# Products between an attention's steps: column pieces of the attention's own shape, or whole 128-column matmuls

## The chip, the cores and the metric

The kernel runs on one core of a Trainium2 chip. A core has TensorE (matrix products, results in PSUM), VectorE, ScalarE, GpSimd and DMA queues, each with its own stream of instructions; semaphores order them. The metric is the device time of one execution in microseconds (us), median of several runs. TensorE's array has 128 rows (the contracted dimension, "active rows") and 128 columns (the outputs, "active columns"). A matmul that needs fewer rows or columns uses a part of the array, and several such matmuls on different parts can run side by side. In this document a *shape* such as 128\*32 is rows\*columns of one matmul, as the profile prints it.

## The reference, cut to what matters

The input is 16 images of 256 channels and 32 x 32 = 1024 positions, all in float32. Each image goes through two layers:

```python
# layer 0: attention with 4 heads of 64
xs = x.reshape(B, C, S).transpose(0, 2, 1)
qkv = (xs @ w_proj + b_proj).reshape(B, S, 4, 192)
q, k, v = jnp.split(qkv, 3, axis=-1)
attn = softmax(einsum('bihd,bjhd->bijh', q, k) * 64 ** -0.5, axis=2)
x = einsum('bijh,bjhd->bihd', attn, v).reshape(B, S, 256) @ w_out + b_out + xs
# layer 1: group norm, attention with 8 heads of 32, group norm, MLP 256 -> 1024 -> 256
x = x + attention(group_norm(x, gn1_w, gn1_b), qkv_w, proj_w, proj_b, phys_bias)
h = group_norm(x, gn2_w, gn2_b)
h = gelu(mlp_w1 @ h + mlp_b1)
x = x + (mlp_w2 @ h + mlp_b2)
```

## The kernel before: the parts that matter

The program runs image after image. An attention is a generator: each step emits the scores of some units (`s`), then weighs the values of the step before (`acc`), and yields; between two steps the caller runs deferred work (`later.tick()`) and, in the second attention, one piece of a list `fill`. D is 64 in the first attention and 32 in the second, and G = 128 / D heads share a tile. Scores contract over D rows, so their shape is 64\*128 or 32\*128 and G of them lie side by side in the array's rows. Weighing contracts over 128 positions and gives D columns, so its shape is 128\*64 or 128\*32, and G of them lie side by side in the columns.

```python
    cols = [P]                                   # P = 128

    def product(o, w, r, **flags):
        for c0 in range(0, P, cols[0]):
            sl = slice(c0, c0 + cols[0])
            nc.tensor.matmul(o[sl], w[:, sl], r, **flags)

    def attention(layer, b, D, qT, kT, v_of, ones_of, scale, project):
        # ... cut: items, units; a step is 6 // G units: 3 in the first attention, 1 in the second
        def scores(i, kb):
            # ... cut: PSUM tiles
            for g in range(G):
                nc.tensor.matmul(
                    tiles[g // 2][:, g % 2, :],
                    kT[g * D : (g + 1) * D, c, kb * P : (kb + 1) * P],
                    qT[g * D : (g + 1) * D, c, t * TB : (t + 1) * TB],
                    start=True,
                    stop=True,
                )
            # ... cut: ScalarE takes the exponentials e of each tile, 128 x 1024

        def weigh(i, kb, es):
            # ... cut
            for g in range(G):
                nc.tensor.matmul(
                    accs[i][g * D : (g + 1) * D, :],
                    v_of(c * G + g, kb),
                    es[g // 2][:, g % 2, :],
                    start=(kb == 0),
                    stop=(kb == SB - 1),
                )
            # ... cut: VectorE sums the exponentials; after the last kb: copy, later.after(2, normalise)

        # ... cut: normalise (matmuls den, shape as acc; then later.after(3, project))
        cols[0] = D
        pending = []
        for step in steps:
            now = [scores(*u) for u in step]
            for p in pending:
                weigh(*p)
            pending = now
            yield
        for p in pending:
            weigh(*p)
        yield
        cols[0] = P
```

So `product` gives one matmul over all 128 columns outside an attention, and 128 / D pieces over D columns inside one. These helpers use it: `out_proj` (profile names `o`, first attention, and `j`, second attention; each has 4 products of 512 moving columns), `group_norm` (`gm`, `gv`, two moving columns), `qkv` (`qk_a`, `v_a` for the first attention, `qk_b`, `v_b` for the second; 4 products of 512 or 8 of 256) and `reduce`, the MLP's second product (`m<-g`, 8 products of 256):

```python
        def reduce(t, co, half):
            n = TB // 2
            ps = wide(f"m2_{b}_{t}_{co}_{half}")[:, 0, :n]
            for hc in range(HC):
                product(
                    ps,
                    k["w2"][:, hc, co * P : (co + 1) * P],
                    gs[t, hc][:, half * n : (half + 1) * n],
                    start=(hc == 0),
                    stop=(hc == HC - 1),
                )
            # ... cut: VectorE adds bias and residual, DMA out
```

The MLP's first product (`m<-hn`) and `qk_b`, `v_b` run outside the attentions, whole. The order of the parts:

```python
    for b in range(B):
        # ... cut: load of the next image
        run(attention_0(b, tiles0, xs[b], ...))
        first_qkv = []
        if b + 1 < B:
            tiles0, first_qkv = qkv_0(b + 1, xs[b + 1])
        run_pieces(first_qkv if b == 0 else hidden)
        later.flush()
        fill = outputs + (first_qkv if b > 0 else [])
        last = NT * CC * SB - 1
        tiles1, second_qkv = qkv_1(b, xn)
        run_pieces(second_qkv)
        # ... cut
        run(
            attention_1(b, tiles1, xs[b], ...),
            {n * last // max(len(fill) - 1, 1): piece for n, piece in enumerate(fill)},
        )
        hidden, outputs = mlp(b, xs[b], hn)
    later.flush()
    run_pieces(hidden + outputs)
```

The second attention has 32 steps (`last` is 31). In it run, for images 1 to 14, the eight `reduce` pieces of the image before and the six pieces of q, k, v of the next image, at steps 0, 2, 4, 7, 9, 11, 14, 16, 19, 21, 23, 26, 28 and 31; image 15 has the eight alone, image 0 none.

Of the kernel before, what the change touches and what calls it, by code (L numbers as in the profile page):

```python
# [14 lines left out]
P = 128  # L15
# [175 lines left out]
def first_pass(ctx, tc, x, out, k):  # L191
    nc = tc.nc
    B, C, S = x.shape
    CC, SB, NT = C // P, S // P, S // TB
# [33 lines left out]

    cols = [P]

    def product(o, w, r, **flags):
        for c0 in range(0, P, cols[0]):
            sl = slice(c0, c0 + cols[0])
            nc.tensor.matmul(o[sl], w[:, sl], r, **flags)  # L236

# [4 lines left out]
    def attention(layer, b, D, qT, kT, v_of, ones_of, scale, project):  # L248
        key = f"{layer}_{b}"
        G = P // D  # L250
        items = [(t, c) for t in range(NT) for c in range(CC)]
        units = [(i, kb) for i in range(len(items)) for kb in range(SB)]
        per = 6 // G
        steps = [units[n : n + per] for n in range(0, len(units), per)]
        res = act.tile([P, CC, S], F32, tag="res", name=f"res_{key}")
        accs, held, sums = {}, {}, {}

        def scores(i, kb):
            t, c = items[i]
            tiles = [wide(f"s_{key}_{i}_{kb}_{n}") for n in range(G // 2)]  # L260
# [8 lines that stand above are left out]
            es = []  # L269
            for n, s in enumerate(tiles):  # L270
                e = work.tile(
                    [P, 2, TB], F32, tag="e", name=f"e_{key}_{i}_{kb}_{n}", bufs=8
                )
                nc.scalar.activation(e, s, AF.Exp, scale=scale)  # L274
                es.append(e)
            return i, kb, es

        def weigh(i, kb, es):
            t, c = items[i]
            if kb == 0:  # L280
                accs[i] = bank(f"acc_{key}_{i}")
# [8 lines that stand above are left out]
            if kb == 0:  # L290
                held[i] = es
                return
            if kb == 1:
                sums[i] = [
                    work.tile([P, 2, TB], F32, tag="es", name=f"es_{key}_{i}_{n}", bufs=4)
                    for n in range(G // 2)
                ]
            for n, e in enumerate(es):
                d = sums[i][n]
                nc.vector.tensor_add(d, held[i][n] if kb == 1 else d, e)  # L300
            if kb == SB - 1:
                r = res[:, c, t * TB : (t + 1) * TB]
                nc.scalar.copy(r, accs.pop(i))
                later.after(2, lambda: normalise(i, r))

        def normalise(i, r):
            t, c = items[i]
            den = bank(f"den_{key}_{i}")
            for g in range(G):
                nc.tensor.matmul(  # L310
                    den[g * D : (g + 1) * D, :],
                    ones_of(c * G + g),
                    sums[i][g // 2][:, g % 2, :],
                    start=True,
                    stop=True,
                )
            at = next(block)
            d = work.tile([P, TB], F32, tag="d", name=f"d_{key}_{i}", bufs=1)
            nc.scalar.activation(  # L319
                d, den, AF.Identity, accum_out=dsum[:, at : at + 1]  # L320
            )
            nc.scalar.activation(
                den, den, AF.Exp, scale=-1.0 / DEN_MIN, accum_out=lsum[:, at : at + 1]
            )
            nc.vector.reciprocal(d, d)  # L325
            nc.vector.tensor_mul(r, r, d)
            if c == CC - 1:
                later.after(3, lambda: project(t, res))

        cols[0] = D  # L330
        pending = []
        for step in steps:
            now = [scores(*u) for u in step]
# [4 lines that stand above are left out]
        for p in pending:  # L338
            weigh(*p)
        yield  # L340
        cols[0] = P


    def out_proj(key, w, nk, src, bias, xs, t, stats):
        ps = wide(f"{key}_{t}")
        for co in range(CC):
            for kc in range(nk):
                product(
                    ps[:, co, :],
                    w[:, kc, co * P : (co + 1) * P],  # L350
                    src(kc),
                    start=(kc == 0),
                    stop=(kc == nk - 1),
                )
        for co in range(CC):
            y = xs[:, co, t * TB : (t + 1) * TB]
            nc.vector.scalar_tensor_tensor(
                y, ps[:, co, :], bias[:, co : co + 1], y, ALU.add, ALU.add
            )
            if stats is not None:  # L360
                nc.vector.bn_stats(stats[:, co, t, :], y)


    def group_norm(key, src, stats, gw, gb, y):
        st = {}

        def means():
            mv = small.tile([P, CC, 2], F32, tag="mv", name=f"mv_{key}")
            for cc in range(CC):
                nc.vector.bn_aggr(mv[:, cc, :], stats[:, cc].rearrange("p t k -> p (t k)"))  # L370
            mean_c = small.tile([P, CC], F32, tag="mean_c", name=f"mean_c_{key}")
            nc.vector.tensor_copy(mean_c, mv[:, :, 0])
            st.update(mv=mv, mean_c=mean_c)
            later.after(1, variances)

        def variances():
            ps = bank(f"gm_{key}")
            product(ps[:, :CC], k["gavg"], st["mean_c"], start=True, stop=True)
            mean = small.tile([P, CC], F32, tag="mean", name=f"mean_{key}")
            nc.vector.tensor_copy(mean, ps[:, :CC])  # L380

            dv = small.tile([P, CC], F32, tag="dv", name=f"dv_{key}")
            nc.vector.tensor_sub(dv, st["mean_c"], mean)
            nc.vector.tensor_mul(dv, dv, dv)
            tv = small.tile([P, CC], F32, tag="tv", name=f"tv_{key}")
            nc.vector.tensor_add(tv, dv, st["mv"][:, :, 1])
            st.update(mean=mean, tv=tv)
            later.after(1, apply)

        def apply():  # L390
            ps = bank(f"gv_{key}")
            product(ps[:, :CC], k["gavg"], st["tv"], start=True, stop=True)
            rstd = small.tile([P, CC], F32, tag="rstd", name=f"rstd_{key}")
            nc.vector.tensor_scalar(rstd, ps[:, :CC], EPS, None, ALU.add)
            nc.gpsimd.tensor_tensor(rstd, rstd, k["mhalf"], ALU.pow)
            a = small.tile([P, CC], F32, tag="ga", name=f"ga_{key}")
            nc.vector.tensor_mul(a, rstd, gw)
            ma = small.tile([P, CC], F32, tag="gma", name=f"gma_{key}")
            nc.vector.tensor_mul(ma, st["mean"], a)
            c = small.tile([P, CC], F32, tag="gc", name=f"gc_{key}")  # L400
            nc.vector.tensor_sub(c, gb, ma)
            for t in range(NT):
                sl = slice(t * TB, (t + 1) * TB)
                for cc in range(CC):
                    nc.vector.tensor_scalar(  # L405
                        y[:, cc, sl], src[:, cc, sl],
                        a[:, cc : cc + 1], c[:, cc : cc + 1], ALU.mult, ALU.add,
                    )

        means()  # L410


    def qkv(key, D, src, weights, b_qk, b_v, v_op, qT, kT, v_dst):
        def qk(ch, which, dst):
            ps = wide(f"qk_{key}_{ch}_{which}")
            for t in range(NT):
                for cc in range(CC):
                    product(
                        ps[:, t, :],
                        weights(cc, which)[:, ch * P : (ch + 1) * P],  # L420
                        src[:, cc, t * TB : (t + 1) * TB],
                        start=(cc == 0),
# [10 lines left out]
        def v(half):  # L433
            ps = wide(f"v_{key}_{half}")
            n = SB // 2
            for i in range(n):
                sb = half * n + i
                o = ps[:, i // 2, (i % 2) * C : (i % 2 + 1) * C]
                for cc in range(CC):
                    product(  # L440
                        o,
                        src[:, cc, sb * P : (sb + 1) * P],
                        weights(cc, 2),
# [75 lines left out]
    def mlp(b, xb, hn):  # L519
# [20 lines left out]
        def reduce(t, co, half):  # L540
            n = TB // 2
            ps = wide(f"m2_{b}_{t}_{co}_{half}")[:, 0, :n]
            for hc in range(HC):
                product(
                    ps,
                    k["w2"][:, hc, co * P : (co + 1) * P],
                    gs[t, hc][:, half * n : (half + 1) * n],
# [371 lines left out]
```

## Time and profile before

| what | value |
|---|---|
| time, median of 3 runs | 4013.07 us (4011.88 to 4015.5) |
| span of the profiled execution | 4013.6 us |
| TensorE busy | 3971.1 us, 99% |
| TensorE records of matmuls | 27957 |
| VectorE, ScalarE busy | 2481.6 us (62%), 2078.1 us (52%) |
| scores of the second attention `s_b`, 4096 records | 624.3 us |
| weighing of the second attention `acc_b`, 4096 records | 546.1 us |
| `s_a`, `acc_a`, 2048 records each | 490.9 us, 477.5 us |

How to read it: a float32 matmul leaves two records. Busy time of a group counts time in which several of its records overlap once, so groups of small shapes have a mean duration well over busy time / count. A row of a timeline merges records of one kind that follow each other: start, time to the end of the last one, engine, line, operation, output<-inputs, shape, size of the moving operand, count. The end of a matmul record is modelled, and the next kind may start before it; the difference of two starts is what an operation holds TensorE for.

### The profile page before, as it was taken

Reading aid. Unit: us, or ns where it says so; the run is one execution under the profiler, and the core shown is the slowest. Engines: PE = TensorE matmul, PEld = TensorE weight load, DVE = VectorE, ACT = ScalarE, POOL = GpSimd, SP = SyncE. Lnnn points to the kernel's source line nnn. Section 1 sums busy time; section 2 is a strip of 40 time slices with the busy share of each in tenths; the row PEclk is TensorE's granted clock in tenths of the full one; section 3 lists DMA queues with packets and bytes.
Section 4 is the critical chain, followed back from the end, with each engine's and each line's share of the span. In section 5 each row is a group of like instructions: output and inputs, shape, how many; then the busy total and the mean of one; then the engine's idle time right before and its main releaser. Section 6 shows DMA issues by size and latency. Waiting matters only on the chain.

```text
span 4013.6 us, 64073 instructions
## 1 busy us (share of the span) xinstructions
PE 3971.1 (99%) x27957; PEld 1518.4 (38%) x27957; DVE 2481.6 (62%) x2538; ACT 2078.1 (52%) x2623; POOL 32.7 (1%) x54
## 2 busy tenths in 40 slices
PE   9999999999999999999999999999999999999998
PEld 3334343343433434334343343433434334343334
DVE  5684756847467474774747747476574765747563
ACT  4564545545455464554545545465454545646462
POOL 1000000000000000000000000000000000000000
PEclk9999999999999999999999999999999999999999
DMA  2000000000000000000000000000000000000000
GB/s 75 1 1 6 17 1 22 1 9 14 1 22 1 9 14 1 22 1 9 14 3 20 1 14 9 3 20 1 22 1 3 20 1 22 1 6 7 1 9 14
DMA packets 19872, 42.07 MB, mean 10 GB/s; under 512 B 5216, under 2 KB 6752, under 8 KB 19584
## 3 DMA queue, kind: packets, MB, share of 16 engines
q1 hardware_dynamic: 13824, 33.56, 2.3%
q8 instruction: 221, 3.62, 0.4%
q10 hardware_dynamic: 5296, 4.20, 0.4%
q14 instruction: 67, 0.55, 0.0%
q0 software_dynamic: 464, 0.15, 0.0%
HBM read 21.12 MB, written 16.78 MB: 9 GB/s over the span
## 4 chain that ended last, share of the span: by engine, by line
PE 94%; DVE 4%; issue 1%; ACT 0%; DMA 0%; POOL 0%; ACTq 0%; POOLq 0%; DVEq 0%
PE s_b L262 14%; PE acc_b L283 12%; PE m L527 11%; PE m L236 11%; PE s_a L262 11%; PE acc_a L283 11%; PE qk_a L236 6%; PE qk_b L236 6%; PE o L236 3%; PE v_b L236 3%; PE v_a L236 3%; PE j L236 3%; PE den_a L310 1%; PE den_b L310 1%; DVE d_a L325 1%
## 5 line engine op out<-in xcount | busy, mean ns | idle before, releaser
L274 ACT ACTIVATE e_b<-s_b 128x1024 f32<-128x1024 f32 x1024 | 994.0, 1025 | 660.6 <-PE s_b L262 648.1
L300 DVE TENSOR_TENSOR es_b<-es_b,e_b 128x1024 f32<-128x1024 f32 x768 | 888.7, 1216 | 147.8 <-ACT e_b L274 146.2
L262 PE MATMUL s_b<-q,k 32*128 32x512 f32 x4096 | 624.3, 640 | 2.8 <-DVE x L552 1.3
L274 ACT ACTIVATE e_a<-s_a 128x1024 f32<-128x1024 f32 x512 | 488.7, 1024 | 205.3 <-PE s_a L262 174.9
L283 PE MATMUL acc_b<-e_b,v 128*32 128x512 f32 x4096 | 546.1, 604 | 0.0
L262 PE MATMUL s_a<-q,k 64*128 64x512 f32 x2048 | 490.9, 608 | 0.0
L300 DVE TENSOR_TENSOR es_a<-es_a,e_a 128x1024 f32<-128x1024 f32 x384 | 467.2, 1217 | 36.0 <-ACT e_a L274 10.2
L527 PE MATMUL m<-hn,w 128*128 128x512 f32 x1024 | 476.1, 606 | 2.0 <-DVE hn L405 2.0
L283 PE MATMUL acc_a<-e_a,v 128*64 128x512 f32 x2048 | 477.5, 600 | 0.0
L236 PE MATMUL m<-g,w 128*32 128x256 f32 (+1 forms) x7808 | 464.9, 379 | 3.7 <-DVE v L448 3.7
L236 PEld LDWEIGHTS m<-g,w 128*32 128x32 f32 (+1 forms) x7808 | 272.6, 111 | 227.7 <-issue 59.3
L262 PEld LDWEIGHTS s_b<-q,k 32*128 32x128 f32 x4096 | 199.3, 183 | 368.4 <-issue 279.2
L535 ACT ACTIVATE g<-m,m1b 128x512 f32<-128x512 f32 x256 | 170.2, 685 | 315.7 <-PE m L527 315.2
L262 PEld LDWEIGHTS s_a<-q,k 64*128 64x128 f32 x2048 | 181.8, 186 | 282.4 <-issue 241.8
L527 PEld LDWEIGHTS m<-hn,w 128*128 128x128 f32 x1024 | 186.6, 191 | 257.1 <-issue 191.5
L448 DVE TENSOR_TENSOR v<-v_b,eones 128x1024 f32<-128x1024 f32 x32 | 39.2, 1224 | 394.4 <-PE v_b L236 394.4
L300 DVE TENSOR_TENSOR es_b<-e_b,e_b 128x1024 f32<-128x1024 f32 x128 | 151.1, 1222 | 188.6 <-ACT e_b L274 188.6
L325 DVE RECIPROCAL d_a<-d_a 128x512 f32<-128x512 f32 x64 | 214.6, 3353 | 83.1 <-ACT d_a L319 83.1
L283 PEld LDWEIGHTS acc_a<-e_a,v 128*64 128x64 f32 x2048 | 132.8, 136 | 322.2 <-issue 317.6
L236 PE MATMUL qk_a<-x,wp 128*32 128x512 f32 (+1 forms) x1856 | 234.3, 594 | 9.1 <-DMA wp<-in_L_conv_w_proj_dram 9.1
L236 PE MATMUL qk_b<-xn,wq 128*128 128x512 f32 x512 | 226.6, 596 | 3.3 <-DVE xn L405 3.3
L283 PEld LDWEIGHTS acc_b<-e_b,v 128*32 128x32 f32 x4096 | 82.5, 108 | 380.2 <-issue 376.0
(104 smaller groups left out, 2389.5 us busy)
## 6 DMA issues: line engine op xcount, KB each, us to landing
x<-in_x_dram SPq DMA_DIRECT2D x32, 512.0 KB, 4.5
out_dram<-x SPq DMA_DIRECT2D x64, 256.0 KB, 2.0
w<-in_L_conv_mlp_w_dram ACTq DMA_DIRECT2D x2, 1024.0 KB, 11.4
wp<-in_L_conv_w_proj_dram ACTq DMA_DIRECT2D x6, 128.0 KB, 8.5
wq<-in_L_conv_qkv_w_dram ACTq DMA_DIRECT2D x1, 768.0 KB, 8.9
wo<-in_L_conv_w_out_dram ACTq DMA_DIRECT2D x1, 256.0 KB, 5.2
wpj<-in_L_conv_proj_w_dram ACTq DMA_DIRECT2D x1, 256.0 KB, 10.6
bv<-in_L_conv_b_proj_dram POOLq DMA_DIRECT2D x1, 128.0 KB, 7.4
```

Of the source, the lines that this page charges most:

```text
L236: nc.tensor.matmul(o[sl], w[:, sl], r, **flags)
L262: nc.tensor.matmul(tiles[g // 2][:, g % 2, :], kT[g * D : (g + 1) * D, c, kb * P : (kb + 1) * P], qT[g * D : (g + 1) * D, c, t * TB : (t + ...
L274: nc.scalar.activation(e, s, AF.Exp, scale=scale)
L283: nc.tensor.matmul(accs[i][g * D : (g + 1) * D, :], v_of(c * G + g, kb), es[g // 2][:, g % 2, :], start=(kb == 0), stop=(kb == SB - 1),)
L300: nc.vector.tensor_add(d, held[i][n] if kb == 1 else d, e)
L310: nc.tensor.matmul(den[g * D : (g + 1) * D, :], ones_of(c * G + g), sums[i][g // 2][:, g % 2, :], start=True, stop=True,)
L325: nc.vector.reciprocal(d, d)
L448: nc.vector.tensor_tensor(v_dst[:, half * n : (half + 1) * n], ps.rearrange("p a (b h d) -> p (a b) h d", b=2, d=D), b_v.unsqueeze(1).to_b ...
L527: nc.tensor.matmul(ps[:, n, :], k["w1"][:, cc, hc * P : (hc + 1) * P], hn[:, cc, t * TB : (t + 1) * TB], start=(cc == 0), stop=(cc == CC - 1),
L535: nc.scalar.activation(g, ps[:, n, :], AF.Gelu, bias=k["m1b"][:, hc : hc + 1])
```

## The change

The helper `product` and its variable `cols` go away, and every product is one matmul over 128 columns, wherever it is emitted. Inside an attention this replaces four matmuls of 32 columns, or two of 64, with one of 128; the pieces, their places between the steps and everything on the other engines stay. It makes the kernel simpler and takes away instructions; in return these products no longer have the shape of the weighing that runs just ahead of them.

```diff
--- before.py
+++ after.py
@@ in first_pass @@
-    cols = [P]
-
-    def product(o, w, r, **flags):
-        for c0 in range(0, P, cols[0]):
-            sl = slice(c0, c0 + cols[0])
-            nc.tensor.matmul(o[sl], w[:, sl], r, **flags)
@@ in attention @@
-        cols[0] = D
         pending = []
         for step in steps:
 ... cut
         yield
-        cols[0] = P
@@ in out_proj @@
             for kc in range(nk):
-                product(
+                nc.tensor.matmul(
                     ps[:, co, :],
                     w[:, kc, co * P : (co + 1) * P],
 ... cut
@@ in group_norm @@
-            product(ps[:, :CC], k["gavg"], st["mean_c"], start=True, stop=True)
+            nc.tensor.matmul(ps[:, :CC], k["gavg"], st["mean_c"], start=True, stop=True)
 ... cut
-            product(ps[:, :CC], k["gavg"], st["tv"], start=True, stop=True)
+            nc.tensor.matmul(ps[:, :CC], k["gavg"], st["tv"], start=True, stop=True)
@@ in qkv, twice @@
-                    product(
+                    nc.tensor.matmul(
 ... cut
@@ in mlp, reduce @@
             for hc in range(HC):
-                product(
+                nc.tensor.matmul(
                     ps,
                     k["w2"][:, hc, co * P : (co + 1) * P],
 ... cut
```

More of the change, by code (lines that the diff above doesn't have):

```diff
@@ L543, in reduce @@
             for hc in range(HC):
-                product(
+                nc.tensor.matmul(
                     ps,
```

## The prediction

> **What bounds the kernel now.** I read the page first. Part 1 and the chain of work that ended last:
>
> ```profile
> PE 3971.1 (99%) x27957; PEld 1518.4 (38%) x27957; DVE 2481.6 (62%) x2538; ACT 2078.1 (52%) x2623; POOL 32.7 (1%) x54
> ...
> PE 94%; DVE 4%; issue 1%; ACT 0%; DMA 0%; POOL 0%; ACTq 0%; POOLq 0%; DVEq 0%
> ```
>
> TensorE is busy 99% of the span and is 94% of the chain; the page's clock row stands at 9 in all 40 slices. So the change is worth what it does to the start-to-start times on TensorE. A busy 99% does not say that the array streams all that time: ends of matmuls are modelled. The groups with shapes kept apart:
>
> ```profile
> L236 PE MATMUL m<-g,w 128*32 128x256 f32 x7680 | 436.7, 379 | 3.7 <-DVE v L448 3.7
> L236 PE MATMUL v_a<-wp,x 128*32 128x256 f32 x1792 | 101.8, 379 | 0.0
> L236 PE MATMUL m<-g,w 128*128 128x256 f32 x128 | 28.2, 380 | 0.0
> ```
>
> The same product `m` occurs split (32 output columns each) and whole (128). A record of either lasts 379 or 380 ns, but the split ones overlap in fours: four take what one whole takes. Each source product gives two records per piece. Then the timeline of TensorE in an image in the middle (start, duration, operation):
>
> ```profile
> 709.66 1.07 PE L283 MATMUL acc_b<-e_b,v 128*32 128x512 f32 x8
> 710.66 1.31 PE L262 MATMUL s_b<-q,k 32*128 32x512 f32 x8
> 711.90 1.07 PE L283 MATMUL acc_b<-e_b,v 128*32 128x512 f32 x8
> 712.78 3.64 PE L236 MATMUL v_a<-wp,x 128*32 128x256 f32 x64
> 716.35 1.14 PE L262 MATMUL s_b<-q,k 32*128 32x512 f32 x8
> ...
> 792.18 3.60 PE L236 MATMUL o<-res_a,wo 128*64 128x512 f32 x16
> 795.61 1.89 PE L283 MATMUL acc_a<-e_a,v 128*64 128x512 f32 x8
> 797.43 1.99 PE L527 MATMUL m<-hn,w 128*128 128x512 f32 x4
> 799.34 1.08 PE L310 MATMUL den_a<-es_a,ones 128*64 128x512 f32 x4
> ...
> 810.08 1.88 PE L527 MATMUL m<-hn,w 128*128 128x512 f32 x4
> 811.80 1.88 PE L236 MATMUL o<-res_a,wo 128*128 128x512 f32 x4
> ```
>
> Two comparisons carry the prediction. acc_b takes 1.00 us to the next start when scores (32*128) follow, but 0.88 when v_a (128*32, its own shape) follows. Four passes of m<-hn between 128*64 neighbours take 1.91 us (797.43 to 799.34), between neighbours of their own shape 1.72 (810.08 to 811.80). A change of the array's shape costs time on the bounding engine.
>
> From single starts in the same trace (medians): within one shape a pass is 429 ns for 512 columns and 216 ns for 256, split or whole alike. acc_b to scores is 543 (114 over 429); acc_a to whole m<-hn is 530 (101 over) and from its first to its second pass 533 (104 over); whole m<-hn to den_a is 523 (94 over); whole v_b to scores 309 (93 over 216), but split v_a or m to scores 329 (113 over). The first acc_b pass after a switch is 453 (24 over), the first acc_a pass 480 (51 over).
>
> **What the Trainium skill says.** "TensorEngine Tiling (Array Packing)", Key Properties: "Changing tiling mode (not just tile) drains the TensorE". The trace agrees: 93 to 114 ns between the last pass of one shape and the first of the next. "TensorE: Matmul & The Clock Gate", section LDWEIGHTS: loading takes P / 1.2 ns, P being columns, so an estimate from that page is 107 ns for 128 columns. The loads' own records last 180 to 190 ns, but the first pass after a switch into 128 columns is late by 104, near the estimate; into 32 columns it is late by 24. Same page, Part 3: tiles run together, some 4 ns apart. Here the four pieces start about 7 ns apart, hence 113 over in place of 93 when split work drains. "Perfetto Trace Analysis", Tensor Engine Instruction, says the end is estimated; so I use starts only.
>
> **The change part by part.** The order of products on every engine stays, tile names apart. Only the products emitted while an attention runs change: one matmul over 128 columns in place of four of 32 (second attention) or two of 64 (first). In the expected order of matmuls these are the m2 pieces (15 images x 8), the q, k, v pieces of the next image (14 x 6), the output projections j (31 of 32) and o (the first of two in each image, 16), and gm_h, gv_h (15 each). TensorE records fall by 5760 + 1344 + 1344 (m, qk_a, v_a) + 384 + 120 (j) + 128 (o) + 60 = 9140, to about 18,800.
>
> *Streaming saves nothing.* 16 passes of 216 ns are 3.46 us whole as split; the last row of the kernel's timeline, 108 whole passes of m<-g in 23.47 us, gives (23.47 - 0.38)/107 = 0.216. The whole weight load (about 190 ns) still fits behind a pass of 216.
>
> *A piece after acc_b or den_b, ahead of scores* (189 of 204). Before: a step ran scores, acc_b, piece, with no switch between acc_b and piece. Now there is one: +114 drain, +104 first load; the exit to scores was a switch already and gets shorter, 93 for 113: -20. Sum +198. Check against the timeline: acc_b to v_a to scores goes from 0.88 + 3.57 = 4.45 us to 1.00 + (16 x 0.216 + 0.104 + 0.093 = 3.65) = 4.65. 189 x 0.198 = 37.4 us. In 14 of them (v_a in the last step) acc_b follows, not scores: the exit is a new switch of 93 + 24 instead of a gain of 20, 14 x 0.137 = 1.9.
>
> *A piece in an attention's first step* (15): scores come ahead of it, so the switch was there. First load 104 for 24, exit -20: +60 each, 0.9 us.
>
> *j in the second attention* (16): +198, 3.2 us. *j in the next image's first attention* (15): +101 + 104 - 7 (split exit to s_a is 530, whole 523) = +198, 3.0 us. *o* (16): acc_a on both sides, so two new switches: 101 + 104 + 94 + 51 = 350, 5.6 us.
>
> *gm_h, gv_h* (30): two columns each. gm_h sits between scores, where switches are already; gv_h waits for VectorE in any case (751 ns after acc_a). Two serial loads of 128 columns for two of 64: an estimate of 40 ns each, 1.2 us.
>
> Sum: 37.4 + 1.9 + 0.9 + 3.2 + 3.0 + 5.6 + 1.2 = 53.2 us. 4013.1 + 53.2 = **4066 us**, 1.3% slower.
>
> **Rivals.** *The added time is absorbed by waits that exist.* In steps without a piece, scores' second half waits for a PSUM buffer that ScalarE frees (pairs 184 ns apart), and ScalarE needs 2 x 1025 ns per step of some 2.24 us. If a later start found that wait already over, up to 0.08 us a piece would return, 15 us in all: 4050. Against it: ScalarE is idle in a step with a piece (3.81 us in front of the exponentials after that v_a), scores right after a piece never wait, and the wait in the next step is on exponentials or evacuations that start with or after those scores. So it shifts along. *Fewer instructions help.* A third of TensorE's records goes; were issue the limit, the split pieces would be slower than whole ones. Both run at 216 ns, so 0; with a hidden gain of 5 ns per pass of some 2,900 passes it would be 15 us, 4051. *A whole load does not hide at 256 columns* just after a switch, so that the second pass is late too: some 75 ns more for the 148 pieces of m and v_a, 11 us, 4077. Against it: after m<-hn's first pass (533) the next is 429 at once. *Both sides of a switch are cheaper than counted*, if acc_b to a whole product behaves like acc_a's 101: 205 x 13 ns = 3 us less. No engine or transfer becomes a new bound: VectorE and ScalarE are at 62 and 52% and get nothing added; DMA is under 5%.
>
> **Range and chances.** The costs are medians with a spread of 1 to 2 ns, taken from the same shapes or from their nearest kin, and the counts follow from the order of instructions; so what is uncertain is absorption (down to -12) and unseen follow-ups (up to +9). 80%: 4054 to 4075. The line of 2% is 4093, which would need a switch worth 0.35 us per piece; faster by 2% has no mechanism. Faster 0.01, within 2% 0.96, slower 0.03.
>
> **What would show it right or wrong.** Right: the matmul group m<-g shows 128*128 x2048 and no 128*32; passes stay at 216 and 429; acc_b to a piece reads 1.00 instead of 0.88 in the timeline, a piece of v or m to scores 3.65 instead of 3.57; acc_a to o 2.73 instead of 2.63, o to acc_a 3.63 instead of 3.43; busy time of VectorE and ScalarE unchanged. Wrong: acc_b to the piece still 0.88 (no drain between these shapes), the piece shorter than 3.5 us, or the step after a piece shorter than 2.24 us (absorption).

## The result, and the profile after

The changed kernel takes 4064.1 us (median of 4 runs, 4062.24 to 4066.24), the kernel before 4013.68 (4 runs). The ratio is 1.0126 with a 95% interval of 1.0108 to 1.0143, that is 50.4 us more (43 to 57). The prediction was 4066 us.

From the page after, part 1 and the chain of work that ended last:

```profile
PE 4023.6 (99%) x18817; PEld 1684.5 (41%) x18817; DVE 2483.7 (61%) x2538; ACT 2080.0 (51%) x2623; POOL 32.7 (1%) x54
...
PE 96%; DVE 2%; issue 1%; ACT 0%; DMA 0%; POOL 0%; ACTq 0%; POOLq 0%; DVEq 0%
```

9140 matmul records are gone, as many as worked out, and TensorE is still busy 99%, 52.5 us longer than before. VectorE and ScalarE have the work they had (2483.7 for 2481.6 us, 2080.0 for 2078.1). The groups of the pieces, shapes kept apart:

```profile
L532 PE MATMUL m<-g,w 128*128 128x256 f32 x2048 | 474.7, 385 | 3.7 <-DVE v L436 3.7
L428 PE MATMUL v_a<-wp,x 128*128 128x256 f32 x512 | 118.5, 385 | 0.0
```

The mean of one record rose from 379 to 385 ns: one pass in 16 follows a switch and is longer by the first load (104 / 16 = 6.5). Busy time adds the two forms of before (m 436.7 + 28.2, and v_a likewise with its first image) and is 10 us over them for m. The rest of the added time stands in no row of these groups, because a drain lies between the last pass of one kind and the first of the next. The timeline of TensorE after, at the same places of the same image as before (start, duration, operation):

```profile
719.12 1.07 PE L273 MATMUL acc_b<-e_b,v 128*32 128x512 f32 x8
720.11 3.72 PE L428 MATMUL v_a<-wp,x 128*128 128x256 f32 x16
723.76 1.14 PE L252 MATMUL s_b<-q,k 32*128 32x512 f32 x8
724.84 1.06 PE L273 MATMUL acc_b<-e_b,v 128*32 128x512 f32 x8
725.83 1.37 PE L252 MATMUL s_b<-q,k 32*128 32x512 f32 x8
727.13 1.07 PE L273 MATMUL acc_b<-e_b,v 128*32 128x512 f32 x8
...
797.51 2.79 PE L273 MATMUL acc_a<-e_a,v 128*64 128x512 f32 x12
800.24 3.70 PE L336 MATMUL o<-res_a,wo 128*128 128x512 f32 x8
803.87 1.94 PE L273 MATMUL acc_a<-e_a,v 128*64 128x512 f32 x8
805.73 1.98 PE L515 MATMUL m<-hn,w 128*128 128x512 f32 x4
```

acc_b to the piece is now 0.99 us (719.12 to 720.11), before 0.88; the piece to scores 3.65, before 3.57. acc_a to o is 2.73, o to acc_a 3.63, acc_a to m 1.86. The scores after a piece and those of the next step last as they did (1.08 us to acc_b, before 1.07; then 1.30 us in both), so nothing is given back there.

A *pass* is one record of a whole matmul, or the two or four records of pieces that run side by side. Starts of single passes after, medians: from one to the next of the same kind it is 216 ns (256 columns) and 429 (512), as before, whole or not. acc_b to whole m 542.5 and to qk_a 543 (429 when split), the first pass of m 320 and of qk_a 533, m to scores 309 (329 when split), qk_a to scores 523 (543), v_a to acc_b 309 (216) with a first acc_b pass of 453 (428). Counted over the trace, passes that end at a change of shape rise from 1453 to 1735, by 282. The parts of the prediction hold 281: the last m piece of image 15 stands ahead of acc_b too, as the 14 v_a pieces do (0.14 us).

### The profile page after: what moved, and what is told of

Read it like the earlier page. It is cut to its first block, busy times and chain, and to the rows that moved or that the text cites. A ratio compares the mean times of both kernels' runs of the same rounds, so it can differ in the third digit from the quotient of the medians.

```text
span 4064.4 us, 45731 instructions
## 1 busy us (share of the span) xinstructions
PE 4023.6 (99%) x18817; PEld 1684.5 (41%) x18817; DVE 2483.7 (61%) x2538; ACT 2080.0 (51%) x2623; POOL 32.7 (1%) x54
## 4 chain that ended last, share of the span: by engine, by line
PE 96%; DVE 2%; issue 1%; ACT 0%; DMA 0%; POOL 0%; ACTq 0%; POOLq 0%; DVEq 0%
PE s_b L252 13%; PE acc_b L273 12%; PE acc_a L273 11%; PE m L515 11%; PE m L532 11%; PE s_a L252 11%; PE qk_a L406 6%; PE qk_b L406 5%; PE v_a L428 3%; PE o L336 3%; PE j L336 3%; PE v_b L428 3%; PE den_a L300 1%; PE den_b L300 1%; DVE es_b L290 1%
## 5 line engine op out<-in xcount | busy, mean ns | idle before, releaser
L532 PE MATMUL m<-g,w 128*128 128x256 f32 x2048 | 474.7, 385 | 3.7 <-DVE v L436 3.7
L532 PEld LDWEIGHTS m<-g,w 128*128 128x128 f32 x2048 | 379.1, 190 | 152.4 <-issue 76.4
L406 PE MATMUL qk_a<-x,wp 128*128 128x512 f32 x512 | 238.1, 609 | 10.4 <-DMA wp<-in_L_conv_w_proj_dram 10.4
## 6 DMA issues: line engine op xcount, KB each, us to landing
w<-in_L_conv_mlp_w_dram ACTq DMA_DIRECT2D x2, 1024.0 KB, 11.8
```

Source lines behind the costliest of these rows:

```text
L406: nc.tensor.matmul(ps[:, t, :], weights(cc, which)[:, ch * P : (ch + 1) * P], src[:, cc, t * TB : (t + 1) * TB], start=(cc == 0), stop=(cc ...
L532: nc.tensor.matmul(ps, k["w2"][:, hc, co * P : (co + 1) * P], gs[t, hc][:, half * n : (half + 1) * n], start=(hc == 0), stop=(hc == HC - 1),)
```

## The experiments

The theory: what costs is a *change of the array's shape* (a switch) at a place in the stream, as a drain of some 100 ns on each side that is new and a first weight load that nothing hides (104 ns for 128 columns, 51 for 64, 24 for 32). The rival: *whole products* cost, each by itself, whatever stands next to them. A second question was whether waits elsewhere take up or give back time.

**Only the projections and norms whole.** The pieces in `fill` stay split.

```diff
 # out_proj, and twice in group_norm
-                product(
+                nc.tensor.matmul(
```

> The kernel before, with only the output projections o and j and the group norms' gm_h and gv_h as whole products; the pieces m, q, k, v stay split. Theory (a change of the array's shape costs a drain and a first weight load, per place): o 16 x 0.350 + j 31 x 0.198 + the norms about 0 = +12 us, so 4026 us. Rival (a whole product is itself slower than its four overlapping parts, so the cost goes with the passes made whole): 376 of 3192 passes, 6 us; weighted by their columns 9 us.

Measured: 4024.52 us, ratio 1.0026 (1.0016 to 1.0036), 10.8 us more (6.4 to 14.4). Near the 12 of the theory, but the interval holds the rival's 9 as well; it leaves out 6 only just. By itself it does not decide.

**The complement: only the pieces whole.**

```diff
 # qkv, twice, and reduce
-                product(
+                nc.tensor.matmul(
```

> The complement: pieces m, q, k, v whole, o, j, gm_h, gv_h split. Theory: 189 x 0.198 + 14 x 0.137 + 15 x 0.060 = +40 us, 4054 us, and with the run of the rest whole it adds up to the whole change (+50). Rival (cost by passes or columns): +41 to +45. This run alone does not tell them apart; the sum does test that the parts are independent.

Measured: 4053.49 us, ratio 1.0096 (1.0080 to 1.0111), 39.8 us more. With the run above it sums to 50.6, the whole change is 50.4: no interaction of the two parts is to be seen, within intervals of 4 to 7 us each way.

**Split, but at the width of the other attention.** No product inside an attention is whole, and none has the shape of its neighbour.

```diff
-        cols[0] = D
+        cols[0] = 96 - D
```

> All products stay split, but at the width of the other attention: 64 columns in the second (whose weighing is 128*32), 32 in the first (128*64). Theory: every place is a change of shape again; the first load is shorter (51 ns for 64 columns, 24 for 32, where whole ones need 104), the exit from 64 columns 100 instead of 93. Per piece 114 + 51 - 13 = 152 ns x 189 = 28.7, last steps 14 x 0.137 = 1.9, first steps 0.2, j second 2.4, j first 15 x 0.138 = 2.1, o 16 x 0.289 = 4.6, norms under 1: +40 us, 4054. Rival (whole 128-column products are the cost, not the change of shape): nothing is whole, so 4014.

Measured: 4052.0 us, ratio 1.0094 (1.0078 to 1.0109), 38.3 us more (31 to 44); the theory said 40, the rival 0. Its timeline of TensorE:

```profile
716.09 1.06 PE L283 MATMUL acc_b<-e_b,v 128*32 128x512 f32 x8
717.09 3.67 PE L236 MATMUL v_a<-wp,x 128*64 128x256 f32 x32
720.69 1.14 PE L262 MATMUL s_b<-q,k 32*128 32x512 f32 x8
...
749.27 2.80 PE L283 MATMUL acc_a<-e_a,v 128*64 128x512 f32 x12
752.00 3.64 PE L236 MATMUL j<-res_b,wpj 128*32 128x512 f32 x32
```

acc_b to v_a takes 1.00 us, as with whole v_a, though two pieces run side by side. acc_a to j takes 2.73, as with whole o, though j here has the very pieces of 32 columns that cost nothing in the second attention. In single starts acc_b to the 64-column m is 543 and its first pass 267 (51 over 216); o's 32-column pieces start with 453. So it is the change that costs, and the first load goes with the width. This refutes the rival.

**Half as many places, same products: pairs of pieces.** Two kernels, whole and split.

```diff
+        pairs = [
+            lambda two=fill[n : n + 2]: [piece() for piece in two]
+            for n in range(0, len(fill), 2)
+        ]
-            {n * last // max(len(fill) - 1, 1): piece for n, piece in enumerate(fill)},
+            {n * last // max(len(pairs) - 1, 1): pair for n, pair in enumerate(pairs)},
```

> The kernel after (whole products), with two pieces at a time in half as many steps (102 places instead of 204). Same products as after. Compared with the split kernel in the same pairs. Theory (cost per place): 87 x 0.198 + 14 x 0.137 + 15 x 0.060 + 12 for o and j = 32 us over the split kernel with pairs, where it was 50 with single pieces. Rival (cost per product): 50 again. Absolute, theory: 102 more steps without a piece, in each of which scores wait some 0.17 us for a PSUM buffer, +17: 4063; rival 4081.

> The kernel before (split products), with two pieces at a time. No place is a change of shape in either form, so only the 102 more steps without a piece count, 0.17 us each: +17 us, 4031.

Measured: whole 4042.07 us (ratio 1.0073, 1.0056 to 1.0090), split 4014.57 (1.0003, 0.9995 to 1.0012). Whole costs 27.5 us over split, not 50. The theory's 32 was 3 too many: in 15 steps j now stands right ahead of a pair and shares its switch (j to qk_a or m 429 ns in the trace), 15 x 0.198 = 3.0, which leaves 29. Where both forms have the same products, the cost falls with the number of places. The timeline of the whole one shows 32 passes behind one switch:

```profile
642.21 1.06 PE L273 MATMUL acc_b<-e_b,v 128*32 128x512 f32 x8
643.21 7.17 PE L532 MATMUL m<-g,w 128*128 128x256 f32 x32
650.31 1.14 PE L252 MATMUL s_b<-q,k 32*128 32x512 f32 x8
```

My second expectation, 17 us for more steps without a piece, was wrong: the split kernel with pairs is 0.7 us slower, within its interval of none. What scores hold TensorE for grew by 2.3 us only (593.7 to 596.0 us). In a stretch without pieces scores take 1.24 to 1.30 us in one step and 1.07 in the next, so they wait in about every second step, not in each.

**More places: q, k, v pieces in halves.** Again whole and split.

```diff
+        def qk_half(ch, which, dst, t):          # one PSUM bank, 2 of the 4 products
+        def v_quarter(part):                     # one PSUM bank, 4 of the 16 products of v
+        if fine:                                 # images 2 to 15
+            return [ ... qk_half ... ] + [lambda part=part: v_quarter(part) for part in range(4)]
```

> The kernel after (whole products), with the q, k, v pieces of images 2 to 15 cut into halves, 84 more places. Theory: each added place costs a change of shape, +0.198, and saves one wait of scores, -0.17: 84 x 0.03 = +2 us, 4067, that is 67 us over the split kernel with the same halves. Rival (cost per product): 50 over it, 4050.

> The kernel before (split products), with the same halves. Added places cost no change of shape; 84 fewer steps in which scores wait 0.17 us: -14 us, 4000.

Measured: whole 4122.2 us (ratio 1.0272, 1.0255 to 1.0290), split 4050.72 (1.0094, 1.0077 to 1.0110). The difference between the forms is 71.5 us, above the 50 of the rival and near the theory's 67. Part of it is the clock (below). Against both expectations the halves themselves slow the kernel down, by a wait ahead of a v piece. The waits of TensorE in the split one:

```profile
PE v_a L236 <- DVE v L485: 34.5, 14, 2.5
```

and the timeline of all engines around one of them:

```profile
710.06 3.35 DVE L325 RECIPROCAL d_b<-d_b 128x512 f32<-128x512 f32 x1
710.43 1.91 PE L236 MATMUL v_a<-wp,x 128*32 128x256 f32 x32
...
716.13 0.68 DVE L485 TENSOR_TENSOR v<-v_a,bv 128x512 f32<-128x512 f32 x1
...
716.87 1.93 PE L236 MATMUL v_a<-wp,x 128*32 128x256 f32 x32 [2.46 <-DVE v L485]
```

The first v piece ends at 712.3, but its evacuation (the sum with the bias that takes it out of PSUM) sits in VectorE's queue behind the reciprocal of 3.35 us, a multiply and two sums of exponentials, and starts at 716.13; the next v piece comes in the very next step and waits for the PSUM buffer. 14 images x 2.46 us = 34.5 us. Here two pieces in steps next to each other run into a slow VectorE operation; the later v pieces, two steps apart and with no reciprocal ahead of their evacuation, show no such wait.

The mean granted clock is 0.993 in the whole kernel and 0.996 in the split one. In some images a stretch of 3.4 us at a clock of 0.5 starts at about the end of this wait or within 1.3 us after it. The v piece behind the wait in the whole kernel, in an image with such a stretch:

```profile
722.69 3.63 PE L465 MATMUL v_a<-wp,x 128*128 128x256 f32 x8 [2.27 <-DVE v L473]
```

The v piece ahead of it takes 1.99 us; here its passes take 427 ns instead of 216. The stretch comes in 12 of the 14 images of the whole kernel and in 5 of the split one, and costs some 1.6 us each time (from that v piece to the third acc_b after it, against images without it): 20 and 8 us. So the split kernel's 36.9 us are 34.5 of waits and 8 of the slower clock, less 5.4 that scores wait less (593.7 to 588.3). And of the 71.5 us between the forms 12 are the clock, while the whole kernel waits 2.8 us less ahead of v (31.7): without both it is some 63 us, an estimate from one trace of each, nearer to the theory's 67 than to 50, and a weaker witness than the pairs.

**The norm one step later.** In the trace before, gm_h splits a row of s_a and waits 0.33 us, and gv_h waits too. This moves them, and gm_g and gv_g of the other norm as well.

```diff
-            later.after(1, variances)
+            later.after(2, variances)
```

> The kernel before, with the norm's first small product one step later, so that gm_h stands behind acc_a and not between two groups of s_a. If changes of shape and the 0.33 us wait in front of gm_h cost what the trace says, scores that take 3.59 us (757.16 to 760.75) fall to 2.78 and gm_h costs about 0.2 at its new place: 15 x 0.6 = -9 us, 4005 us. Rival: the wait moves with it (VectorE ends last), -2 us or none.

Measured: 3992.31 us, ratio 0.9944 (0.9930 to 0.9957), 21.4 us less, over twice what I expected. The timeline before, and after it that of this kernel:

```profile
757.16 1.13 PE L262 MATMUL s_a<-q,k 64*128 64x512 f32 x4
758.62 0.28 PE L236 MATMUL gm_h<-mean_c_h,gavg 128*64 128x2 f32 x4 [0.33 <-ACT den_a L322]
758.83 1.99 PE L262 MATMUL s_a<-q,k 64*128 64x512 f32 x8
760.75 2.79 PE L283 MATMUL acc_a<-e_a,v 128*64 128x512 f32 x12
763.70 0.28 PE L236 MATMUL gv_h<-tv_h,gavg 128*64 128x2 f32 x4 [0.15 <-DVE tv_h L386]
```

```profile
755.02 2.85 PE L262 MATMUL s_a<-q,k 64*128 64x512 f32 x12
757.79 2.79 PE L283 MATMUL acc_a<-e_a,v 128*64 128x512 f32 x12
760.42 0.23 PE L236 MATMUL gm_h<-mean_c_h,gavg 128*64 128x2 f32 x4
760.58 2.85 PE L262 MATMUL s_a<-q,k 64*128 64x512 f32 x12
763.36 2.79 PE L283 MATMUL acc_a<-e_a,v 128*64 128x512 f32 x12
765.98 0.23 PE L236 MATMUL gv_h<-tv_h,gavg 128*64 128x2 f32 x4
```

Scores fall from 3.59 us with gm_h between them to 2.77; over the trace s_a holds TensorE 9.0 us less (483.9 to 474.9). What I had not counted: acc_a 6.3 less (460.6 to 454.3), since gv_h's wait is gone as well (acc_a to gv_h 751 to 429 ns, 15 x 0.32 = 4.8), m<-hn 6.1 less (gv_g 2.0 less, but gm_g 2.0 more). Of m<-hn's, the wait ahead of gv_g (558 to 429) is 1.9. Another 2.8 is one place per image where the next weight load waits for ScalarE's evacuation: there, before, a pass takes 512 and the next 533 ns although the shape stays, 15 x 0.187. So a wait can expose a first load without any change of shape. The last 1.4 lie in the last image, where fewer passes ran at half clock (853 ns).

**On top of the later norm, three kernels:** q and k in halves (v whole as a piece), the first of the MLP's products m<-hn in each image split into 64 columns, and all products whole.

```diff
 # first MLP product split: in hidden, around the products of one hc
+                cols[0] = D0 if t == 0 and hc == 0 else P
-                    nc.tensor.matmul(
+                    product(
+                cols[0] = P
```

> Split products, the norm one step later, and only q and k of images 2 to 15 in halves (v whole as a piece, so that no v piece waits for VectorE). 56 more places, which cost nothing in shape. If what made the halves slow was the wait of 2.46 us in front of the second v piece (14 times, 34.5 us), and the scores' waits fall as they did there (593.7 to 588.3 us), this is 3992 - 4 = 3988 us. If halves cost by themselves (a second ScalarE evacuation, more issue), over 3995.

> Split products, the norm one step later, and the first of the MLP's products m<-hn in each image split into 64 columns as well: it stands between acc_a and den_a, both 128*64. Theory: acc_a to m (101 + 104) and m to den_a (94 + 51) are no changes of shape any more: 15 x 0.350 = -5.2 us, 3987 us. Rival (only whole against split matters, or the change is hidden there): 3992.

> The kernel after (whole products) with the norm one step later. If the norm's wait and the changes of shape at the pieces are independent, this is 50 us over the split kernel with the same norm, 3992 + 50 = 4042 us. If the later norm had gained by removing a change of shape that the whole kernel pays twice, the difference would be under 50.

Measured: halves 3996.72 us (0.9960, 0.9946 to 0.9973), first product split 3988.34 (0.9936, 0.9923 to 0.9950), all whole 4050.71 (1.0093, 1.0077 to 1.0108). Halves without the v wait still gain nothing (the second case of the expectation, over 3995): scores hold TensorE 4.3 us longer than with the later norm alone (594.0 to 598.3), not shorter. Why their waits moved that way is open. Splitting the first MLP product took out what it should at its place: acc_a to m 430 and m to den_a 429 in single starts, where it was 530 and 523. The time is 4.0 us under the later norm alone, for 5.2 expected; the two intervals overlap, so times alone do not separate 3992 from 3988. It is the lowest time here, 25 us under the kernel before.

All whole with the later norm is 58.4 us over split with the later norm, not 50 and not under it. That is the theory at two more places: gm_h and gv_h now stand behind acc_a with no wait that hides a switch, and whole they take 529 + 133 + 181 ns from the last acc_a pass to scores, split 429 + 163. 30 x 0.25 = 7.5, and 50.4 + 7.5 = 57.9.

## Why the prediction was right

**Streaming saves nothing.** Shown: passes stay at 216 and 429 ns, and a third of TensorE's records less gives no time back.

**A piece after acc_b or den_b.** The drain of 114 was taken from acc_b to scores, as in the kernel before no whole product follows acc_b; it measured 113.5 to 114. First load 104, exit 20 less: all as read. The run with only the pieces whole has 39.8 us, for 37.4 + 1.9 + 0.9 = 40.2 predicted. That the drain goes with the change, and the load with the width, is shown by the split at the other width.

**Projections.** 11.8 us predicted with o and j, 10.8 measured together with the norms.

**The norms were the one step that failed,** a small one. "gv_h waits for VectorE in any case (751 ns after acc_a)" was taken as a fixed wait, and both norms as +40 ns. After the change gm_h's part, from s_a over gm_h to s_a, rose by 100 ns (two passes 133 apart and 181 to scores, for 79 and 134), while the wait ahead of gv_h shrank from 751 to 561, so that its part fell by 90. The sum is 0.15 us instead of 1.2. The trace after shows why, on VectorE:

```profile
765.95 3.35 DVE L315 RECIPROCAL d_a<-d_a 128x512 f32<-128x512 f32 x1 [0.50 <-ACT d_a L309]
769.22 0.10 DVE L368 COPY mean_h<-gm_h 128x2 f32<-128x2 f32 x1
771.34 0.16 DVE L374 TENSOR_TENSOR tv_h<-dv_h,mv_h 128x2 f32<-128x2 f32 x1
771.55 0.38 PE L380 MATMUL gv_h<-tv_h,gavg 128*128 128x2 f32 x2
```

mean_h, which reads gm_h, stands behind the reciprocal, so tv_h starts 5.39 us after the reciprocal's start before and after alike, and the 100 ns that gm_h takes longer cost nothing. That is 100 of the 190 ns by which the wait shrank; the other 90 are that gv_h starts 0.31 us after tv_h's start when split and 0.22 when whole, and why is open. This is the absorption that the prediction named as a rival for scores and left out here. It explains 1 of the 2 to 3 us by which the prediction was high; the rest is within the interval.

**The rivals.** Absorption at scores: none, s_b holds TensorE 593.7 us before and after. Fewer instructions: no gain. A second pass made late by the load: no, m's second pass after a switch is at 216. My picture of scores' waits (0.17 us in each step without a piece), which the prediction did not need, failed in the three sets of runs that leaned on it.

## What to carry to other kernels

When small products of another kind are put between tiled matmuls on a TensorE that sets the end, count the places where the array's shape changes, and read the cost of one from starts in the trace (here 0.2 us where a product brings one more change, 0.35 where it brings two). Splitting a product to its neighbour's shape cost no streaming time here, as its parts ran side by side (216 and 429 ns per pass either way); grouping products behind one switch is the other way (27.5 us instead of 50). And look at what tiny products wait for: two columns of a norm, placed one step too early, cost more than a third of what this whole change did.

## What was not expected

The later norm is worth 21.4 us where the sum from the trace gave 9, since the early product brought more waits than the one that was counted, and two changes of shape (passes that end at a change of shape fall from 1453 to 1423, two per image for 15 images). Halved pieces, free on TensorE by count, cost 36.9 us because a reciprocal of 3.35 us on VectorE held the evacuation that they needed (34.5 us of waits), and stretches at half clock followed some of these waits (8 us). Doubling up pieces leaves the time as it was (0.7 us, interval -2 to +5).
